# State space layer: softplus chain moved up by two to three turns; recurrent, distance and last layers' tiles turned by TensorE's transposing operation

## The chip, the cores and the metric

The kernel runs on one core of one Trainium2 chip. A core has five engines that run their own instruction streams: TensorE (PE in the profile, with its weight loads as PEld), VectorE (DVE), ScalarE (ACT), GpSimd (POOL) and SyncE (SP, which here only issues DMAs). SBUF is the working memory of 128 partitions, PSUM the memory that TensorE writes. The metric is the device time of one execution in microseconds (us).

## The reference

The model has four layers, each of which mixes tokens ("conv") and then works on each token ("ffn"), with a residual around both. The input x is 4 x 64 x 128 x 128 in float32; a row of 128 channels is a token. These are the parts that the change touches:

```python
# layers 0 and 2, ffn: a recurrence over all 8192 tokens of an image
Wx = einsum('bti,hi->bth', x, W)              # then batch norm over all tokens
yt = sigmoid(wx_t + yt @ V.T)                 # one step; scan over t
# layer 1, conv: distances between the rows of each image, from q = x - mean
score = -(q2[..., :, None] + k2[..., None, :] - 2.0 * einsum('bdnl,bdml->bdnm', q, k))
# layer 2, conv: a selective state space model, 128 channels x 16 states
dt = softplus(einsum('blr,dr->bld', dt, dt_proj_w) + dt_proj_b)
h = exp(dt_t * A) * h + (dt_t * x_t) * B_t    # one step; scan over all positions
y = einsum('bds,bs->bd', h, C_t)
# layer 3: pooled tokens for a graph (conv); a router over 64 experts (ffn)
logits = einsum('bsd,ed->bse', x, gate_w) + gate_b
```

Every one of these parts normalises the tokens first (mean and variance over the 128 channels), and the sums over channels need the tile with channels on the partitions, which is why tiles are turned.

## The kernel before, in words

**Turning a tile.** A token tile has 128 tokens on the partitions and 128 channels beside each other. The kernel turns it by a matmul of the tile, as the stationary operand, with the identity `env.ident`: the result in PSUM is the transposed tile. In float32 such a matmul is two passes over the array, so each call leaves two matmuls and two weight loads in the trace. Elsewhere the kernel already calls `transpose`, which leaves one of each (L541 and L623 of layer 0's mixer, L3405 and others of layer 3).

**Recurrent layers (0 and 2), `rnn_ffn`, L1157.** First the input pass, `rnn_inputs` (L1051): 16 blocks of 16 tiles. A block is loaded by SP, DVE takes the statistics, ACT, POOL and DVE scale the tiles, PE turns four tiles into one PSUM tile `pt` (`turn`, L1120) and multiplies four tiles with themselves into `gram` (`square`, L1126), and ACT copies `pt` to `xn`. Each buffer has two copies (`DEEP = 2`), so the load of a block waits until the last scaling of the block before last has read its buffer. Then the recurrence: the 8192 tokens of an image are cut into 128 chunks of 64 steps that run side by side, after 16 steps that warm the state up. A step computes z = xn[t] wt + state vt (L1233 and L1235, 512 columns each), ACT takes the sigmoid (L1239), and `give` (L1257) turns the four tiles of the state before (L1260), which DVE adds to the residual (L1261). On PE `give(t - 1)` stands between the matmuls of step t and those of step t + 1.

**The planner.** `rnn_inputs`, `l1_distances`, `l3_nodes` and the token pass of `l3_layer` write no order themselves: `Plan.step` (L66) is told an engine, a duration, what a step reads and writes and which buffers it takes, and `Plan.emit` (L94) lists the steps. For each engine it takes the first listed step that can start when the engine is free, by the durations it was told; the order that comes out is then fixed for PE, ACT, DVE and POOL. A changed duration can so change the order.

**Distances, `l1_distances`, L1700.** 16 blocks of 16 tiles: statistics, scaling, `turn` (L1790), copy to `xT` (L1797), then products of each turned tile with itself (L1806) on top of a diagonal (L1803), and the sum on DVE (L1813).

**State space layer, `l2_conv`, L2270.** 64 chunks of 512 positions x 2 images. The order is written out by hand in turns: turn t holds the scan of one pair of states (`one_state`, L2768 on DVE and the product gs, L2773 on POOL); a chunk has 32 turns. In a turn come first `decay` (da on ACT, for the scan three turns later), `spread` (bs on PE, every second turn), `fetch` (two cc DMAs on SP, every fourth turn), `inputs` (bs x dx on DVE, for the next turn), then the scan and gs; then the steps that `at(turn, ...)` has put on this turn; last, every second turn, `summed` (py on PE), for gs of five and six turns before. The steps of chunk n's projection are put on the 32 turns before the chunk is scanned, t0 = 32 (n - 1). The softplus chain is among them: `steps` (PE, L2589) and `parts` (ACT, L2593 and L2594) at t0 + 15 and 16, then

- `exp` (ACT, L2597), `one_more` (two on ACT, L2601 and L2602, which write w and less), `log` (ACT, L2605, in place on w),
- `lost` (POOL, L2608: e - less), `add_lost` (POOL, L2611: up + e), `size` (POOL, L2620: dt = w + up), `scaled` (POOL, L2623: dx = dt x xs),
- `twice(b, "dt")` and `twice(b, "dx")` (L2617): four DMAs on SP each, which lay the first (b = 0) or second image's half out for the scan. The first `inputs` of the chunk, on turn t0 + 31, needs dx of b = 0.

PE, ACT, DVE and POOL keep the order as written; the order of SP's DMAs is not written out. Other steps on the same turns: the previous chunk's `layer1` (PE, t0 + 18 and 21) and `hidden` (ACT, L2675, t0 + 19 and 22), `gelu` (ACT, t0 + 24).

**Last layer, `l3_layer`, L3109.** 16 blocks in the token pass: PE mixes four rows (L3170), DVE adds them to the loaded block (L3175) and takes statistics, POOL stores the block, the tiles are scaled into `xq` (L3189 and L3191), turned (`turn`, L3198), copied (L3204), multiplied with the gate (L3210) and written as logits by ACT (L3220). `l3_nodes` (L2880) turns one pooled tile for each of its 16 blocks (L2919).

Of the kernel before, what the change touches and what calls it, by code (L numbers as in the profile page):

```python
# [23 lines left out]
B, H, W, C = 4, 64, 128, 128  # L24
# [1026 lines left out]
def rnn_inputs(env, x, xn, gram):  # L1051


    nc, tc = env.nc, env.tc
    V, S, T, G = nc.vector, nc.scalar, nc.tensor, nc.gpsimd
    NB, DEEP = 16, 2
    with tc.tile_pool(name="rs", bufs=DEEP) as sb, tc.tile_pool(name="rp", bufs=3, space=PSUM) as psum:
        deep = ["xt", "st", "mv", "rs", "nb", "d", "t", "xl"]
        plan = Plan(dict(pt=3, **{n: DEEP for n in deep}), " ".join(deep))
        step = plan.step  # L1060

        def block(b, l0):
            v = {}
            plan.block()

            def load():
                v["xt"] = sb.tile([P, NB, C], F32, name="xt")
                nc.sync.dma_start(v["xt"], x[b, :, l0 : l0 + NB, :])

            def stats(j):  # L1070
                def f():
                    if j == 0:
                        v["st"] = sb.tile([P, NB, 2, 3], F32, name="st")
                    for q in range(j, j + 4):
                        V.bn_stats(v["st"][:, q].rearrange("p s k -> p (s k)"), v["xt"][:, q, :])
                return f

            def merge():
                d, v["mv"] = sb.tile([P, NB], F32, name="d"), sb.tile([P, NB, 2], F32, name="mv")
                mean, sq, mv = v["st"][:, :, :, 1], v["st"][:, :, :, 2], v["mv"]  # L1080
                V.tensor_sub(d, mean[:, :, 0], mean[:, :, 1])
                V.tensor_add(mv[:, :, 0], mean[:, :, 0], mean[:, :, 1])
                V.tensor_add(mv[:, :, 1], sq[:, :, 0], sq[:, :, 1])
                V.scalar_tensor_tensor(d, d, 0.25 * C, d, ALU.mult, ALU.mult)
                V.tensor_add(mv[:, :, 1], mv[:, :, 1], d)
                V.tensor_scalar(mv[:, :, 1], mv[:, :, 1], 1.0 / C, env.eps5, ALU.mult, ALU.add)

            def guess():
                v["rs"] = sb.tile([P, NB], F32, name="rs")
                S.activation(v["rs"], v["mv"][:, :, 1], AF.Ln)  # L1090
                S.activation(v["rs"], v["rs"], AF.Exp, scale=-0.5)
                if b == 0 and l0 == 0:
                    S.preload_act_table_set("natural_log_exp_and_others")

            def refine():
                r, t = v["rs"], sb.tile([P, NB], F32, name="t")
                V.tensor_mul(t, v["mv"][:, :, 1], r)
                V.scalar_tensor_tensor(t, t, -0.5, r, ALU.mult, ALU.mult)
                V.scalar_tensor_tensor(r, t, 1.5, r, ALU.add, ALU.mult)
                v["nb"] = sb.tile([P, NB], F32, name="nb")  # L1100
                V.scalar_tensor_tensor(v["nb"], v["mv"][:, :, 0], -0.5, r, ALU.mult, ALU.mult)

            def scale(eng, *js):
                def f():
                    if "xl" not in v:
                        v["xl"] = sb.tile([P, NB, C + 1], F32, name="xl")
                        G.memset(v["xl"][:, :, C : C + 1], 1.0)
                    for j in js:
                        r, n = v["rs"][:, j : j + 1], v["nb"][:, j : j + 1]
                        if eng is S:  # L1110
                            S.activation(v["xl"][:, j, 0:C], v["xt"][:, j, :], AF.Identity, bias=n, scale=r)
                        else:
                            eng.tensor_scalar(v["xl"][:, j, 0:C], v["xt"][:, j, :], r, n, ALU.mult, ALU.add)
                return f

            def turn(j0, w):
                def f():
                    w["pt"] = psum.tile([P, 4, P], F32, name="pt")
                    for j in range(4):
                        T.matmul(w["pt"][:, j, :], v["xl"][:, j0 + j, 0:C], env.ident, start=True, stop=True)  # L1120
                return f

            def square(j0):
                def f():
                    for j in range(j0, j0 + 4):
                        T.matmul(gram, v["xl"][:, j, 0:C], v["xl"][:, j, :], start=False, stop=False)  # L1126
                return f

            step("sp", 0.1, "", "xt", load, new="xt", late=4.0)
            for j in range(0, NB, 4):  # L1130
                step("dve", 1.15, "xt", "st", stats(j), new="st" if j == 0 else "")
            step("dve", 1.2, "st", "mv d", merge, new="mv d")
            step("act", 0.5, "mv", "rs", guess, new="rs")
            step("dve", 0.8, "mv rs", "rs nb t", refine, new="nb t")
            for j0 in range(0, NB, 4):
                w = {}
                if j0 % 8 == 0:
                    step(
                        "dve", 0.7, "xt rs nb" + " xl" * (j0 > 0), "xl" * (j0 == 0) + " xv%d" % j0, scale(V, j0, j0 + 4),
                        new="xl" if j0 == 0 else "",  # L1140
                    )
                step("pool", 0.5, "xt rs nb xl", "xp%d" % j0, scale(G, j0 + 3))
                step("act", 1.0, "xt rs nb xl", "xm%d" % j0, scale(S, j0 + 1, j0 + 2))
                ready = "xl xv%d xp%d xm%d" % (j0 - j0 % 8, j0, j0)
                step("pe", 1.0, ready, "pt", turn(j0, w), new="pt")
                step("pe", 1.05, ready, "", square(j0))
                step("act", 0.6, "pt", "", lambda j0=j0, w=w: S.copy(xn[:, l0 + j0 : l0 + j0 + 4, b, :], w["pt"]))

# [8 lines left out]
def rnn_ffn(env, x, out, w, vt, gamma, beta):  # L1157
# [4 lines left out]
    with tc.tile_pool(name="rc", bufs=1) as cp:  # L1162
# [63 lines left out]
        with tc.tile_pool(name="rw", bufs=4) as sb, tc.tile_pool(name="rx", bufs=4) as xp, tc.tile_pool(  # L1226
# [26 lines left out]
            def recurrence():  # L1253

                xt, state = None, start

                def give(t, done):  # L1257
                    pt = tp.tile([P, B, C], F32, name="pt")
                    for b in range(B):
                        nc.tensor.matmul(pt[:, b, :], done[:, b, :], env.ident, start=True, stop=True)  # L1260
                    nc.vector.tensor_add(xt[:, :, t % NO, :], xt[:, :, t % NO, :], pt)  # L1261
                    if t % NO == NO - 1:
                        for b in range(B):
                            nc.gpsimd.dma_start(ov[b, :, t + 1 - NO : t + 1, :], xt[:, b])

                for t in range(L):
                    new = last if t == L - 1 else sb.tile([P, B, NCH], F32, name="state")
                    sigmoid(new, cell(t, state))
                    if t > 0:
                        give(t - 1, state)  # L1270
                    if t % NO == 0:
                        xt = xp.tile([P, B, NO, C], F32, name="xo")
                        for b in range(B):
                            nc.sync.dma_start(xt[:, b], xv[b, :, t : t + NO, :])
                    state = new
                give(L - 1, last)
# [423 lines left out]
def l1_distances(env, x, dscr, keys):  # L1700
# [6 lines left out]
    with tc.tile_pool(name="dc", bufs=1) as cp, tc.tile_pool(name="ds", bufs=DEEP) as sb, tc.tile_pool(  # L1707
# [9 lines left out]
        def block(i):  # L1717
# [68 lines left out]
            def turn(j0, w):  # L1786
                def f():
                    w["pt"] = psum.tile([P, 4, P], F32, name="pt")
                    for j in range(4):
                        T.matmul(w["pt"][:, j, :], v["xl"][:, j0 + j, :], env.ident, start=True, stop=True)  # L1790
                return f

            def keep(j0, w):
# [476 lines left out]
def l2_conv(env, x, out, prm):  # L2270
# [14 lines left out]
    with ExitStack() as ctx:  # L2285
# [99 lines left out]
        def at(turn, *steps):  # L2385
            turns.setdefault(turn, []).extend(steps)
# [125 lines left out]
        def project(n, t0):  # L2512
# [124 lines left out]
            at(t0 + 13, lambda: part(N))  # L2637
            at(t0 + 15, steps)
            at(t0 + 16, parts)
            at(t0 + 17, exp)  # L2640
            at(t0 + 18, one_more)
            at(t0 + 19, lost)
            at(t0 + 20, log, load_res)
            at(t0 + 21, add_lost)
            at(t0 + 23, size, lambda: twice(0, "dt"))
            at(t0 + 26, scaled, lambda: twice(0, "dx"))
            at(t0 + 33, lambda: twice(1, "dt"))
            at(t0 + 34, lambda: twice(1, "dx"))

# [230 lines left out]
def l3_nodes(env, x, xl, poolT):  # L2880
# [4 lines left out]
    with tc.tile_pool(name="ns", bufs=DEEP) as sb, tc.tile_pool(name="np", bufs=2, space=PSUM) as psum:  # L2885
# [4 lines left out]
        def block(g, w0):  # L2890
# [25 lines left out]

            def turn():
                v["pt"] = psum.tile([P, P], F32, name="pt")
                T.matmul(v["pt"], v["p"], env.ident, start=True, stop=True)  # L2919

            def keep():
                S.activation(poolT[:, w0 // NB, g * P : g * P + P], v["pt"], AF.Identity, scale=1.0 / 16)
# [186 lines left out]
def l3_layer(env, x, out, cv, ff):  # L3109
# [7 lines left out]
    with ExitStack() as ctx:  # L3117
# [36 lines left out]
        with tc.tile_pool(name="go", bufs=DEEP) as sb, tc.tile_pool(name="gp", bufs=2, space=PSUM) as psum:  # L3154
# [4 lines left out]
            def block(g, w0):  # L3159
# [34 lines left out]
                def turn(w):  # L3194
                    def f():
                        w["pt"] = psum.tile([P, 4, P], F32, name="pt")
                        for j in range(4):
                            T.matmul(w["pt"][:, j, :], w["xq"][:, j, :], env.ident, start=True, stop=True)  # L3198
                    return f

                def keep(w):
# [33 lines left out]
                for j in range(0, NB, 4):  # L3235
# [1 line left out]
                    step("dve", 0.4, "xt y%d rs nb" % j, "xq xv", scale(V, w, j, 0), new="xq")  # L3237
                    step("pool", 1.0, "xt y%d rs nb xq" % j, "xp", scale(G, w, j, 1, 2))
                    step("act", 0.5, "xt y%d rs nb xq" % j, "xm", scale(S, w, j, 3))
                    step("pe", 1.2, "xq xv xp xm", "pt", turn(w), new="pt")  # L3240
                    step("act", 0.6, "pt", "xT", keep(w), new="xT")
                    step("pe", 1.0, "xT", "pl", gate(w), new="pl")
                    step("act", 1.0, "pl", lgn, logits(j, w), new=lgn if w0 + j == 0 else "")
# [268 lines left out]
```

## Time and profile before

| | us |
|---|---|
| three runs | 11602.66, 11594.26, 11613.55; median 11602.66 |
| the profiled execution | 11600.68 |
| its span, first to last instruction | 11598.8 |

Busy time over the span: DVE 9891.4 us (85%), ACT 7224.5 (62%), PE 6752.8 (58%), POOL 5633.8 (49%). Stages, in us from the span's start: input pass and recurrence of layer 0 about 1370 to 1720, distances 1727 to 1958, state space layer 6430 to 10550, input pass and recurrence of layer 2 about 10555 to 10905, last layer's token pass 11167 to 11460.

How to read it: a row of a timeline gives start, length, engine, line, operation, the tiles written and read, shapes and how many were merged into the row; in brackets stands how long the engine had been idle and what it waited for. Matmuls are pipelined and their ends are modelled, so how fast PE works is read from starts, not from busy time. "SPq" is SP issuing a DMA; the landing is seen in who waits for it. PEclk is the share of TensorE's clock that was granted.

### The profile page before, as it was taken

The numbers are of one execution on the slowest core, as the hardware profiler recorded it, in microseconds if no ns is written. First come the engines' busy times: TensorE is split into PE (matmuls) and PEld (weight loads), VectorE is DVE, ScalarE is ACT, GpSimd is POOL, SyncE is SP. The second block draws the span as 40 slices with busy tenths as digits, with TensorE's granted clock in tenths as the row PEclk, the third lists the DMA queues.
The fourth block names the chain that finished last, engine by engine and source line by source line (L and its number), as shares of the span: only waits on it lengthen the run. The fifth ranks groups of instructions, "written<-read, shape, count | busy, mean of one in ns | idle before, by whom it ended". The sixth has DMA issues, their size and how long they took to land. (4 is left out here: it accounts for less than half of the span.)

```text
span 11598.8 us, 117532 instructions
## 1 busy us (share of the span) xinstructions
PE 6752.8 (58%) x34862; PEld 4019.9 (35%) x34862; DVE 9891.4 (85%) x16377; ACT 7224.5 (62%) x9683; POOL 5633.8 (49%) x4762
## 2 busy tenths in 40 slices
PE   7877696000000000008999688888888888888675
PEld 5665564000000000007888233333333333335343
DVE  7567637999999999998998599999999999996444
ACT  4244434888886777743333587787788778775332
POOL 1000016999990000002332488888888888883322
PEclk8877798555555555559999788888888888888887
DMA  5312245111111111111111344444444444443444
GB/s 194 99 40 48 70 148 142 56 57 58 57 65 47 55 55 55 51 48 52 46 47 34 80 111 115 117 110 120 113 113 118 110 116 120 110 113 102 171 140 151
DMA packets 794209, 1059.52 MB, mean 91 GB/s; under 512 B 243564, under 2 KB 460878, under 8 KB 779982
## 3 DMA queue, kind: packets, MB, share of 16 engines
q1 hardware_dynamic: 749630, 925.61, 27.8%
q0 software_dynamic: 34368, 124.14, 3.2%
q8 instruction: 280, 4.59, 0.2%
q14 instruction: 379, 3.10, 0.1%
q10 hardware_dynamic: 9552, 2.08, 0.1%
HBM read 682.39 MB, written 251.71 MB: 81 GB/s over the span
## 5 line engine op out<-in xcount | busy, mean ns | idle before, releaser
L2773 POOL TENSOR_TENSOR gs<-hist,cc 128x512 f32<-128x512 f32 x2048 | 2586.7, 1272 | 659.9 <-DVE hist L2768 494.7
L2768 DVE TENSOR_TENSOR_SCAN hist<-da,state,bs 128x512 f32<-128x512 f32 x1984 | 2517.5, 1269 | 0.0
L1693 PE MATMUL pm<-ident,m 128*1 128x128 f32 x1 | 0.4, 372 | 3191.3 <-DMA pk<-spare 3191.3
L2729 ACT ACTIVATE da<-dt,am 128x512 f32<-128x512 f32 x2048 | 1420.6, 719 | 377.0 <-DVE hist L2768 320.9
L2760 DVE TENSOR_TENSOR bs<-dx,bs 128x512 f32<-128x512 f32 x2048 | 1380.8, 674 | 159.8 <-DMA dx<-dx 150.3
L1501 POOL TENSOR_TENSOR diff<-key 128x2048 f32<-128x2048 f32 (+11 forms) x364 | 1384.1, 3854 | 86.1 <-DVE key L1506 74.4
L2784 PE MATMUL py<-gs,both 128*64 128x512 f32 x4096 | 1253.1, 693 | 0.0
L1693 PEld LDWEIGHTS pm<-ident,m 128*1 128x1 f32 x1 | 0.1, 79 | 3191.4 <-issue 3191.4
L1523 ACT COPY keep<-rank 128x1536 int16<-128x1536 int16 (+11 forms) x364 | 612.8, 1686 | 437.5 <-DVE rank L1525 388.6
L1919 POOL IOTA row<- 72x1 int32 x1 | 0.1, 135 | 1769.8 <-ACTq L1868 1769.8
L1499 ACT COPY low<-key 128x2048 f32<-128x2048 f32 (+11 forms) x364 | 627.7, 1725 | 284.0 <-DVE key L1506 275.8
L1524 DVE COPY_PREDICATED rank<-back,rank 128x1536 int16<-128x1536 uint8 (+11 forms) x364 | 781.3, 2146 | 16.7 <-ACT keep L1523 16.7
L1525 DVE COPY_PREDICATED rank<-back,keep 128x1536 int16<-128x1536 uint8 (+11 forms) x364 | 777.8, 2137 | 12.5
L1506 DVE TENSOR_TENSOR key<-low,key 128x2048 f32<-128x2048 f32 (+11 forms) x364 | 744.4, 2045 | 12.4
L1505 DVE TENSOR_TENSOR key<-low,key 128x2048 f32<-128x2048 f32 (+11 forms) x364 | 749.0, 2058 | 6.3 <-DMA key<-dist 3.9
L2739 PE MATMUL bs<-bt,pick 96*128 96x512 bf16 x1024 | 435.1, 425 | 497.7 <-DVE hist L2768 492.3
L1502 ACT ACTIVATE turned<-diff 128x2048 int8<-128x2048 f32 (+11 forms) x364 | 600.4, 1699 | 36.6 <-DMA key<-dist 26.8
L1514 ACT ACTIVATE back<-turned 128x3072 uint8<-128x3072 int8 (+12 forms) x182 | 582.2, 3199 | 0.0
L2218 PE MATMUL pe<-ew,xg 128*128 128x128 f32 x4096 | 506.3, 277 | 0.0
L2218 PEld LDWEIGHTS pe<-ew,xg 128*128 128x128 f32 x4096 | 490.2, 194 | 4.0
L2784 PEld LDWEIGHTS py<-gs,both 128*64 128x64 f32 x4096 | 218.6, 146 | 693.7 <-issue 258.8
L2739 PEld LDWEIGHTS <-pick 96*128 96x128 bf16 x1024 | 98.9, 97 | 970.7 <-issue 970.7
(840 smaller groups left out, 17726.8 us busy)
## 6 DMA issues: line engine op xcount, KB each, us to landing
cc<-cd SPq DMA_DIRECT2D x1024, 256.0 KB
xt<-state SPq DMA_DIRECT2D x64, 1024.0 KB
dt<-dt SPq DMA_DIRECT2D x512, 128.0 KB
dx<-dx SPq DMA_DIRECT2D x512, 128.0 KB
xo<-state SPq DMA_DIRECT2D x128, 256.0 KB
state<-xo POOLq DMA_DIRECT2D x128, 256.0 KB, 2.8
xl<-in_L_ffn_weight SPq DMA_DIRECT2D x32, 1024.0 KB
tk<-in_x SPq DMA_DIRECT2D x32, 512.0 KB
```

Source lines behind the costliest of these rows:

```text
L1499: nc.scalar.copy(c, l)
L1501: nc.gpsimd.tensor_sub(d, lo[part], hi[part])
L1505: nc.vector.tensor_tensor(lo[part], c, hi[part], ALU.min)
L1506: nc.vector.tensor_tensor(hi[part], c, hi[part], ALU.max)
L1524: nc.vector.copy_predicated(l, t, h)
L1525: nc.vector.copy_predicated(h, t, kv)
L2218: T.matmul(w["pe"][:, j, :], w["xg"][:, q, j, :], ew[:, q, :], start=False, stop=(j == 3 and q == E - 1))
L2729: nc.scalar.activation(da, x_["dt%d" % b][:, s % 2, :], AF.Exp, scale=am[:, s : s + 1])
L2760: nc.vector.tensor_mul(live["db", t], x_["dx%d" % b][:, s % 2, :], live["bs", t - s % 2])
L2768: nc.vector.tensor_tensor_scan(h, live.pop(("da", t)), live.pop(("db", t)), 0.0 if first else state[b][:, s : s + 1], ALU.mult, ALU.add,)
L2773: nc.gpsimd.tensor_tensor(gs, h, live.pop(("cc", t)), ALU.mult)
L2784: nc.tensor.matmul(x_["py%d" % b][h * H : h * H + H], both, live.pop(("gs", t - 1 + h)), start=False, stop=(s == S - 1),)
```

## The change

Five turning matmuls become `transpose` calls with the same operands. In two places the planner is told a shorter duration for them: 0.55 for 1.0 in `rnn_inputs`, 0.7 for 1.2 in the last layer's token pass; in the distances and for the pooled tiles the told durations stay. In the state space layer seven compute steps of the softplus chain and the first image's copies move to earlier turns: `one_more` from 18 to 17, `lost` from 19 to 18, `log` from 20 to 18, `add_lost` from 21 to 20, `size` and the copies of dt from 23 to 21, `scaled` and the copies of dx from 26 to 23. `load_res` stays on turn 20, and the second image's copies on 33 and 34.

```diff
@@ rnn_inputs
-                        T.matmul(w["pt"][:, j, :], v["xl"][:, j0 + j, 0:C], env.ident, start=True, stop=True)
+                        T.transpose(w["pt"][:, j, :], v["xl"][:, j0 + j, 0:C], env.ident)
...
-                step("pe", 1.0, ready, "pt", turn(j0, w), new="pt")
+                step("pe", 0.55, ready, "pt", turn(j0, w), new="pt")
@@ rnn_ffn, give
-                        nc.tensor.matmul(pt[:, b, :], done[:, b, :], env.ident, start=True, stop=True)
+                        nc.tensor.transpose(pt[:, b, :], done[:, b, :], env.ident)
@@ l1_distances
-                        T.matmul(w["pt"][:, j, :], v["xl"][:, j0 + j, :], env.ident, start=True, stop=True)
+                        T.transpose(w["pt"][:, j, :], v["xl"][:, j0 + j, :], env.ident)
@@ l2_conv, project
             at(t0 + 16, parts)
-            at(t0 + 17, exp)
-            at(t0 + 18, one_more)
-            at(t0 + 19, lost)
-            at(t0 + 20, log, load_res)
-            at(t0 + 21, add_lost)
-            at(t0 + 23, size, lambda: twice(0, "dt"))
-            at(t0 + 26, scaled, lambda: twice(0, "dx"))
+            at(t0 + 17, exp, one_more)
+            at(t0 + 18, log, lost)
+            at(t0 + 20, load_res, add_lost)
+            at(t0 + 21, size, lambda: twice(0, "dt"))
+            at(t0 + 23, scaled, lambda: twice(0, "dx"))
@@ l3_nodes
-                T.matmul(v["pt"], v["p"], env.ident, start=True, stop=True)
+                T.transpose(v["pt"], v["p"], env.ident)
@@ l3_layer
-                            T.matmul(w["pt"][:, j, :], w["xq"][:, j, :], env.ident, start=True, stop=True)
+                            T.transpose(w["pt"][:, j, :], w["xq"][:, j, :], env.ident)
...
-                    step("pe", 1.2, "xq xv xp xm", "pt", turn(w), new="pt")
+                    step("pe", 0.7, "xq xv xp xm", "pt", turn(w), new="pt")
```

## The prediction

> **What bounds the kernel now.** I read the stage view first (busy time, TensorE clock and DMA share of stretches), because each part of the change lives in a stage with a limit of its own. The rows are the recurrent layer's input pass, its recurrence, the distances, the state space layer and the last layer's token pass; the columns are PE, PEld, DVE, ACT and POOL busy time with instruction counts, clock, DMA share, GB/s.
>
> ```profile
> 1370.00:1511.00 141.00, 120.87 (x1022) 118.32 (x1023) 94.14 (x482) 93.25 (x227) 30.34 (x80) 0.92 0.34 120
> 1554.00:1720.00 166.00, 164.53 (x762) 104.57 (x760) 45.23 (x67) 43.28 (x63) 32.56 (x61) 1.00 0.49 171
> 1727.00:1958.00 231.00, 179.16 (x1152) 140.16 (x1152) 173.95 (x579) 96.84 (x228) 117.81 (x145) 0.93 0.60 160
> 6430.00:10550.00 4120.00, 3457.98 (x13447) 1429.71 (x13448) 3903.41 (x4788) 3210.12 (x4705) 3352.23 (x3200) 0.86 0.43 112
> 11167.00:11460.00 293.00, 206.79 (x786) 119.79 (x786) 177.37 (x581) 139.60 (x296) 81.20 (x154) 0.85 0.42 153
> ```
>
> PE alone is full in the recurrence (164.5 of 166 us), DVE alone in the state space layer (3903 of 4120). In the other three nothing is full, so they turn on loops between engines. The recurrence and the input pass come twice in the kernel.
>
> Next I asked what DVE waits for in the state space layer (total us, times, longest):
>
> ```profile
> DVE bs L2760 <- DMA dx<-dx: 150.3, 55, 46.4
> DVE bs L2760 <- PE bs L2739: 9.2, 15, 1.8
> ```
>
> One wait stands out: 46.4 us once, at the start, and 103.9 us over 54 later chunks, 1.9 us each. The timeline of one chunk shows where it comes from (start, length, engine, line, operation, wait):
>
> ```profile
> 7998.99 1.28 POOL L2773 TENSOR_TENSOR gs<-hist,cc 128x512 f32<-128x512 f32 x1 [0.49 <-PE pa L2670]
> ...
> 8002.13 2.36 POOL L2608 TENSOR_TENSOR e<-e,less 128x1024 f32<-128x1024 f32 x1
> 8006.91 2.35 POOL L2611 TENSOR_TENSOR up<-up,e 128x1024 f32<-128x1024 f32 x1
> 8011.81 2.36 POOL L2620 TENSOR_TENSOR dt<-w,up 128x1024 f32<-128x1024 f32 x1
> 8014.14 3.72 POOL L2773 TENSOR_TENSOR gs<-hist,cc 128x512 f32<-128x512 f32 x3
> 8017.83 2.35 POOL L2623 TENSOR_TENSOR dx<-dt,xs 128x1024 f32<-128x1024 f32 x1
> 8020.21 2.39 SPq L2617 DMA_DIRECT2D dx<-dx  x4
> 8023.20 0.69 DVE L2760 TENSOR_TENSOR bs<-dx,bs 128x512 f32<-128x512 f32 x1 [2.21 <-DMA dx<-dx]
> ```
>
> POOL ends dx at 8020.18, its copies land 3.02 us later, and DVE has idled since 8020.99.
>
> Last, one step of the recurrence, and a group that already uses the transposing operation:
>
> ```profile
> 1603.34 1.02 PE L1235 MATMUL z<-state,vt_sb 128*128 128x512 f32 x2
> 1604.20 1.05 PE L1260 MATMUL pt<-ident,state 128*128 128x128 f32 x8
> 1604.40 0.69 ACT L1239 ACTIVATE state<-z,bias 128x512 f32<-128x512 f32 x1 [1.92 <-PE z L1235]
> 1605.09 1.02 PE L1233 MATMUL z<-xn,wt 128*128 128x512 f32 x2
> ```
>
> ```profile
> 475.96 0.60 PE L623 MATMUL p<-ident,om 128*49 128x128 f32 x4
> ```
>
> Four turning matmuls are eight passes, 0.89 us (1604.20 to 1605.09), 0.111 each. Four transposing operations are four passes; with 0.272 us for one (the least duration at L623), (0.60 - 0.272) / 3 = 0.109 us from one to the next. So a turned tile costs half.
>
> **The change part by part.** All sums go against the profiled execution: span 11598.8, time 11600.7, which is 2 us under the median shown.
>
> *Recurrence (twice).* A step lasts 2.61 us (1603.34 to 1605.95, the next z<-state). It loses four passes: 4 x 0.111 = 0.445, leaving 2.165. The cover is the sigmoid: it ends at 1605.09 and its reader starts at 1605.95, 0.86 us of slack, of which 0.41 remain. The same loop without turning, in the warm-up steps, runs at 1.90 us (1536.52, 1538.42, 1540.32), below 2.165; so PE stays the limit. DVE's addition (0.69 us) and the loads and stores (DMA share 0.49, going to 0.59) fit. Gain 64 x 0.445 x 2 layers = 57 us. Bounds: the only four 128-column transposes in a row, of a strided source at L3405, take 0.75 us, so (0.75 - 0.284) / 3 = 0.155 each and a gain of 35; 0.109 gives 58. I take 57, since L1260 reads whole rows.
>
> The Trainium skill ("TensorE: Matmul & The Clock Gate", Terms) calls the transposing mode four times faster for FP32. By that a tile would cost 0.222 / 4 = 0.055 us and the two recurrences would gain 85. The row at 475.96 shows a factor of two.
>
> *State space layer.* Nothing is added; instructions change places. On ACT, L2601 and L2602 now follow L2597 without the da between, and L2605 comes two turns earlier, ahead of the four L2675. The three start 0.94 and 1.07 apart from 7996.83, so "less" ends at 8000.0. On POOL the first step now stands behind gs of turn 18 (ends 8000.27), so it starts there and doesn't wait. From it to dx there stood, in issue spacing, the steps 2.32 + 2.31 + 2.33, seven gs at 1.23 and a state copy of 0.14: 15.7 us. Now five gs and two copies stand between: 6.96 + 6.11 + 0.28 = 13.35. So dx starts at 8013.6 and ends at 8016.0, 4.2 us earlier; it lands at 8019.0, 2.0 before DVE is free. The 2.2 us wait goes.
>
> What each queue is moved past: SP issues the four dt copies (2.43 us) as POOL ends dt, now at 8011.0, and the cc fetch behind them waits for POOL's state copy at 8013.6 anyway, then dx at 8016.0: no collision. load_res keeps its turn. ACT's da for turn 21 now stands behind L2601 and L2602 and ends at 8000.6 against 7998.5; its scan starts at about 8002.9, so 2.3 us of lead remain, and the next two da lose one L2605 (1.06). The first L2675 group moves back by as much, and with it PE's second layer1, which waits for its bank; the bs behind that is asked for four turns later. POOL is up to 5.9 us behind DVE after dx where it was 4.7; PE waits for gs (5 turns of 1.77 later), so bs comes later. From a gs to the bs it can hold up lie eight turns, 14.2 us; gs, two py matmuls of 0.86 and bs need about 5, so POOL may lag 8 to 9 us before DVE feels it. Late next on DVE is nothing: scans follow at 1.77 us (8012.34, 8014.10, 8015.88). Gain 104 (the 103.9 us); the first 46.4 is a chain without scans between and stays. Bounds: 50, if half the wait returns by a late da or bs; 115, if the ACT wait for dt (48.7 us in 63) also counted.
>
> *Input pass (twice).* PE falls from 7.1 to 5.3 us per block of 7.5, but PE is not the loop: the load of a block is issued when the last scaling by ACT frees its buffer (ACT 1431.28 + 0.88, SP 1432.22), DVE waits for it (0.64), and so on over two blocks, 15.04 us. The planned duration 0.55 for 1.0 changes the written order: the planner's turn now ends before ACT's second scaling does, so ACT's first copy precedes the third scaling and the second the fourth. One more copy stands ahead of the last scaling, 0.46 us (1438.34 to 1438.80) per loop, 8 loops, 2 layers: +7.4. The tail of 16 tiles saves 1.8 each: -3.6. I take +4; bounds -10 (a third of the 33 us that ACT's copies wait for PE) and +10.
>
> *Distances.* The order stays. DVE waits 10.6 us for the products and 35.7 for loads. I take -4 (tail 1.8, 2 of the waits); bounds -14 and +10 (five more clock windows of 3.4 us at half speed).
>
> *Last layer.* SP's load waits for ACT's scaling, which stands behind copies that wait for PE; each block loses 0.445 us there, some 11 blocks: -5. Bounds -30 (half of the 53.7 us that DVE waits for loads) and +10 (the new order puts one 0.58 us copy ahead in 16 blocks). The 16 pooled tiles lie beside DMA: 0.
>
> Sum: -57 - 104 + 4 - 4 - 5 = -166; 11600.7 - 166 = 11435.
>
> **The rivals.**
> *Half the wait returns* in the state space layer (dx late by SP's order, or da late in turns 21 to 23): 11600.7 - 166 + 52 = 11487. For it: the margins are 2.0 and 2.3 us. Against: every step's cover has a row.
> *The turned tiles cost as before* (the transposing form of a whole tile gives nothing): 11435 + 57 = 11492. Against it: one pass per call at L623 and L541.
> *POOL's lag stops DVE* (slower): the four long steps now fall within 16 us on POOL, gs slips, PE's py waits, the bs behind it comes late. It decides once DVE waits over 162 / 63 = 2.6 us per chunk, which needs POOL's lag beyond some 11 us at turn 24; at 4 us per chunk the time is 11435 + 252 = 11687. For it: PE already waits 234.6 us for gs. Against: the lag I work out is 5.9.
> *The clock falls* where transposes replace matmuls, if they count for nothing: the passes then take twice as long, PE becomes the limit, and a block needs 10.7 us for 7.5 in the input passes (3.2 x 15 x 2 = 96), 17.5 for 13 in the distances (4.5 x 15 = 68), 17.2 for 15 in the last layer (2.2 x 16 = 35); 11435 + 199 = 11634. Against it: from 324.4 to 327.8 us, 16 of 20 matmuls are transposes of L623, and the granted clock is 1.00 there and through 331.2. In the recurrence matmuls alone fill 1.72 of 2.165 us.
> By the Trainium skill (the same page, Part 4: PE-mode transpose) transposing doesn't count as PE-busy and full clock does not engage; the clock at 324.4 speaks against that.
>
> **How the numbers follow.** Chances: the forecast 0.76, half the wait 0.10, tiles as before 0.03, POOL's lag 0.06, the clock 0.03, nothing measurable 0.02. The forecast's own range is 11385 to 11475 (its bounds: all gains at their best give -215). Taking in the two cases near 11490 makes 11385 to 11500, with over 8 in 10. Faster 0.89, within 0.2% (23 us, what a measurement here can tell) 0.02, slower 0.09.
>
> **What would show it.** Right: recurrence steps of 2.16 us with four passes at L1260; no row of DVE waiting for dx but the first; first scans of successive chunks 58.3 us apart, where they are 60.8 now in three chunks of four. Wrong: DVE waiting for bs from PE or scans waiting for da; steps of 2.6; a clock under 0.9 in the input pass.

## The result and the profile after

| | before | after |
|---|---|---|
| median, us | 11601.4 (11594.26 to 11613.55) | 11411.9 (11396.1 to 11417.72) |
| profiled execution, us | 11600.68 | 11396.1 |
| its span, us | 11598.8 | 11394.3 |

The ratio is 0.9833, 95% interval 0.9816 to 0.985: 190 us faster between the medians, where 166 were forecast. The time 11411.9 lies 23 us under the forecast 11435 and inside the forecast's own range of 11385 to 11475.

The stage view of the changed kernel (stretch in us, its length, then PE, PEld, DVE, ACT, POOL busy with instruction counts, granted clock, DMA share, GB/s); the stretches are the input pass and the recurrence of layer 0, the distances, the state space layer, and the last layer's token pass:

```profile
1367.50:1511.50 144.00, 98.24 (x764) 93.17 (x765) 94.08 (x480) 93.99 (x226) 31.49 (x80) 0.86 0.33 118
1554.00:1692.00 138.00, 136.40 (x508) 72.31 (x506) 44.87 (x66) 43.77 (x64) 32.28 (x61) 1.00 0.58 206
1699.50:1928.00 228.50, 164.11 (x896) 118.93 (x896) 174.00 (x579) 95.36 (x228) 118.47 (x145) 0.87 0.60 161
6402.00:10430.00 4028.00, 3450.62 (x13452) 1427.75 (x13452) 3910.02 (x4794) 3206.46 (x4706) 3351.12 (x3200) 0.87 0.45 114
11014.00:11258.00 244.00, 168.68 (x531) 80.44 (x530) 173.23 (x581) 141.32 (x296) 83.03 (x154) 0.87 0.51 184
```

The limits are where they were: PE is full in the recurrence (136.4 of 138), DVE in the state space layer (3910 of 4028), nothing elsewhere. Two lengths stand out: the recurrence's stretch is 28 us shorter, and the token pass takes 244 us where it took 293.

One step of the recurrence in the changed kernel (start, length, engine, line, operation):

```profile
1599.90 1.02 PE L1235 MATMUL z<-state,vt_sb 128*128 128x512 f32 x2
...
1600.76 0.60 PE L1260 MATMUL pt<-ident,state 128*128 128x128 f32 x4
...
1602.06 1.02 PE L1235 MATMUL z<-state,vt_sb 128*128 128x512 f32 x2
```

Four passes instead of eight, and 2.16 us from one step to the next (1599.90 to 1602.06), where it was 2.61.

What DVE waits for in the state space layer now (us in total, times, longest):

```profile
DVE bs L2758 <- DMA dx<-dx: 46.7, 3, 45.4
DVE res L2693 <- PE pn L2686: 25.4, 16, 14.5
...
DVE bs L2758 <- PE bs L2737: 5.9, 11, 1.6
```

The wait for dx is there once, at the start (45.4), and 1.3 us besides; before it was 46.4 and 103.9.

From the first and last instruction of each stage in the two profiled executions:

| part | forecast | measured |
|---|---|---|
| recurrence, two layers | -57 | -28.4 and -28.3 |
| state space layer | -104 | -95.5 (4125.3 to 4029.8) |
| input pass, two layers | +4 | +3.4 and -0.5 |
| distances | -4 | -2.1 |
| last layer | -5 | -51.8 (422.5 to 370.7) |
| pooled tiles | 0 | -1.2 |

In these two executions the change is 204 us, where it is 190 between the medians. Four terms came out about as worked out (recurrence, input pass, distances, pooled tiles). The last layer gained ten times its term, and the state space layer lost something the working did not contain.

### The profile page after: what moved, and what is told of

The parts are those of the page before. It is cut to its first block, busy times and chain, and to the rows that moved or that the text cites. A ratio compares the mean times of both kernels' runs of the same rounds, so it can differ in the third digit from the quotient of the medians.

```text
span 11394.3 us, 114467 instructions
## 1 busy us (share of the span) xinstructions
PE 6576.2 (58%) x33310; PEld 3832.9 (34%) x33310; DVE 9893.7 (87%) x16377; ACT 7223.3 (63%) x9683; POOL 5638.0 (49%) x4762
## 5 line engine op out<-in xcount | busy, mean ns | idle before, releaser
L2758 DVE TENSOR_TENSOR bs<-dx,bs 128x512 f32<-128x512 f32 x2048 | 1382.0, 675 | 53.2 <-DMA dx<-dx 46.7
```

What stands on the lines that cost most here:

```text
L2758: nc.vector.tensor_mul(live["db", t], x_["dx%d" % b][:, s % 2, :], live["bs", t - s % 2])
```

## The experiments

The theory for the state space layer and the recurrence is that of the prediction. For the last layer there are two: A, the shorter told duration changes the written order of the token pass and the order makes the gain; B, the faster turning makes it.

### The softplus chain alone

```diff
 (the kernel before, with these turns only)
-            at(t0 + 23, size, lambda: twice(0, "dt"))
-            at(t0 + 26, scaled, lambda: twice(0, "dx"))
+            at(t0 + 21, size, lambda: twice(0, "dt"))
+            at(t0 + 23, scaled, lambda: twice(0, "dx"))
...
```

> The kernel before with the moved softplus chain alone. If the chain alone makes the whole change of the state space layer (its stretch went from 4125.3 to 4029.8 us in the two profiles shown), this kernel is 95 us faster, ratio 0.992, and the layer's stretch is 4030 us. If the other edits help the layer from outside (its first wait, the clock), it gains less than 80 us. If the prediction's 104 us were lost to a wait for the moved steps, DVE waits for bs or da in this trace; if they were lost in the statistics chunks (every fourth), those chunks are 70.0 us apart and the others 58.5.

Measured: 11494.16 us, ratio 0.9904 (0.9889 to 0.992). From the layer's first scan to its last it took 3908.2 us, for 4006.4 before and 3911.7 in the changed kernel: the chain alone makes the change of this layer, 98 us. The time fell by 114; of the rest, 11 us lie in the first stage, which the edit does not touch. First scans of successive chunks are 58.5 us apart (60.8 before; 58.3 were forecast), but in every fourth chunk, which takes the statistics of the next group, it is 69.9 (68.5 before; all medians). Over the layer, the 48 other chunks gave 111 us, and the 15 statistics chunks cost 13, 0.9 us each on the mean. In the changed kernel it is 109 and 14.

Where the 0.9 us go is seen on POOL and DVE in the same 8 us of the changed kernel, first POOL and then DVE:

```profile
8069.57 2.51 POOL L2771 TENSOR_TENSOR gs<-hist,cc 128x512 f32<-128x512 f32 x2
8072.02 0.19 POOL L2773 COPY state<-hist 128x4 f32<-128x4 f32 x1
8072.17 2.35 POOL L2623 TENSOR_TENSOR dx<-dt,xs 128x1024 f32<-128x1024 f32 x1
8074.48 2.48 POOL L2771 TENSOR_TENSOR gs<-hist,cc 128x512 f32<-128x512 f32 x2
```

```profile
8070.89 1.23 DVE L2414 TENSOR_TENSOR d<-st 128x16 f32<-128x16 f32 x1
8072.04 0.21 DVE L2415 TENSOR_TENSOR mv<-st 128x16 f32<-128x16 f32 x1
8072.17 2.39 DVE L2416 TENSOR_TENSOR v<-st 128x16 f32<-128x16 f32 x1
8074.49 1.28 DVE L2417 SCALAR_TENSOR_TENSOR d<-d 128x16 f32<-128x16 f32 x1
8075.81 1.19 DVE L2418 TENSOR_TENSOR v<-v,d 128x16 f32<-128x16 f32 x1
8077.03 0.23 DVE L2419 TENSOR_SCALAR v<-v,eps 128x16 f32<-128x16 f32 x1
```

DVE's operations on 16 numbers per partition last as long as the POOL operation beside them: L2416 begins with dx at 8072.17 and ends at 8074.56, dx at 8074.52. Over the layer, 71 of these operations begin while POOL is idle and take 0.18 us on the mean; 89 begin while a POOL operation runs and take 1.18; the long ones end within 0.03 us (median) of a start or end of a POOL operation. Meanwhile bs (L2758), which reads one operand from PSUM, keeps its 0.675 us. The six merging operations take 5.64 us from first start to last end in the changed kernel (4.12 before), since POOL's backlog now covers their turn; the four refining ones take 1.67 (2.63 before), since it no longer covers theirs: together 0.6 us more. DVE's wait for the residual (L2693 <- PE) grew from 21.3 to 25.4 us over the whole layer, in waits of some 0.3 us in 12 of the statistics chunks, 0.3 per chunk. These two are the 0.9 us.

By the Trainium skill ("SBUF — State Buffer", Who interferes with whom), a VectorE instruction with two SBUF inputs and a GpSimd instruction that reads SBUF exclude each other for a whole instruction, and one with at most one SBUF input, outside VectorE's two-port modes, goes free. The trace agrees, with 1.18 against 0.18 us. It is a rule that spoke against this change, and the prediction did not weigh it.

### The recurrence alone

```diff
-                        nc.tensor.matmul(pt[:, b, :], done[:, b, :], env.ident, start=True, stop=True)
+                        nc.tensor.transpose(pt[:, b, :], done[:, b, :], env.ident)
```

> The kernel before with the transposing operation in the two recurrences alone. By the prediction's working: 57 us faster, 28.5 us for each recurrence, steps of 2.165 us, ratio 0.995. By the rule of a fourth of the price for float32: 85 us, steps of 1.94. If a step is held by ACT's sigmoid or DVE's addition once PE is shorter, it stays above 2.3 us and the gain is under 40 us.

Measured: 11547.81 us, ratio 0.9952 (0.9937 to 0.9967), so 60 us; the stages are 28.3 and 29.6 us shorter. Steps, in this kernel's trace:

```profile
1605.43 1.02 PE L1235 MATMUL z<-state,vt_sb 128*128 128x512 f32 x2
1606.29 0.60 PE L1260 MATMUL pt<-ident,state 128*128 128x128 f32 x4
1607.59 1.02 PE L1235 MATMUL z<-state,vt_sb 128*128 128x512 f32 x2
```

2.16 us. The factor of two holds and PE stays the limit; the factor of four is refuted for these tiles.

### The last layer: order alone, operation alone

```diff
 (order alone)
-                    step("pe", 1.2, "xq xv xp xm", "pt", turn(w), new="pt")
+                    step("pe", 0.7, "xq xv xp xm", "pt", turn(w), new="pt")
 (operation alone)
-                            T.matmul(w["pt"][:, j, :], w["xq"][:, j, :], env.ident, start=True, stop=True)
+                            T.transpose(w["pt"][:, j, :], w["xq"][:, j, :], env.ident)
```

> The kernel before with the last layer's told duration 0.7 for 1.2 alone: the tiles are still turned by matmul, only the written order of the token pass changes. Theory A (the order carries the gain: loads of tiles and ACT's scalings stand ahead of other work): the last layer's stretch falls by some 45 of the 52 us, ratio 0.996. Theory B (the shorter turning carries it): the stretch stays within 5 us, ratio 1.000. Theory C (both are needed): under 15 us here and under 15 us with the transposing operation alone, and 52 us only together.

> The kernel before with the transposing operation in the last layer's token pass alone, told duration 1.2 kept: the order on every engine is that of the kernel before. Theory A (order): the last layer's stretch falls by 5 us or less, as the prediction had it. Theory B (speed of the turning): it falls by some 45 us, ratio 0.996. Theory C (both are needed): under 15 us.

Measured: the order alone gives 11566.45 us, ratio 0.9965 (0.9951 to 0.9978), and the last layer's stage is 38 us shorter. The operation alone gives 11603.48, ratio 0.9996 (0.9987 to 1.0005), and the stage is 8 us shorter. A holds: the order carries three quarters of the gain, with tiles turned as slowly as ever.

How it does so is a matter of buffers. A block of 16 tiles sits in one of three buffers from its load until its last scaling, and the load of the third next block waits for that scaling. In the kernel before, around the load of block 7, which takes the buffer of block 4 (SP's issue of a weight load, POOL's store of block 6, POOL's scalings, SP's load of the tile, DVE's first addition of the loaded block):

```profile
11245.37 0.38 SPq L3378 DMA_DIRECT2D xl<-in_L_ffn_weight  x1
...
11246.36 0.58 POOL L3179 DMA_DIRECT2D out<-xt  x1 [7.61 <-DVE xq L3191]
11246.98 2.63 POOL L3191 TENSOR_SCALAR xq<-xt,rs,nb 128x128 f32<-128x128 f32 x6
...
11247.88 0.32 SPq L3165 DMA_DIRECT2D xt<-state  x1
...
11257.26 1.28 DVE L3175 TENSOR_TENSOR xt<-xt,ps 128x512 f32<-128x512 f32 x2 [5.53 <-DMA xt<-state]
```

The last scaling of block 4 is the second in POOL's row of six. It ends at 11247.85 (ACT's last one at 11247.38), and the load follows at once. In the written order this scaling stands behind the store of block 6, and the store needs all four additions of block 6; DVE's own last scaling of block 4 stands behind the fourth of them (11245.38), too. So each load waits until the block loaded before it has been added to completely. The load lands 9.3 us later, and DVE idles 5.53 us for it. The same block with the order alone changed:

```profile
11246.38 0.32 SPq L3165 DMA_DIRECT2D xt<-state  x1
...
11248.17 0.58 POOL L3179 DMA_DIRECT2D out<-xt  x1 [1.56 <-PE pt L3198]
...
11251.43 0.69 DVE L3175 TENSOR_TENSOR xt<-xt,ps 128x512 f32<-128x512 f32 x1 [1.75 <-POOL xq L3191]
```

POOL's last scaling of block 4 now stands ahead of the store of block 6 and ended at 11240.62. DVE's stands behind the second addition of block 6, not the fourth. ACT's is the last, at 11246.31, and the load follows it. It lands 4.9 us after its issue, at 11251.31. DVE waits for it here as well: the row names POOL's scaling only because that ended last, at 11251.39. Over the first 13 blocks, the ones whose buffer a later load takes, POOL's scaling is the last in 11 before, and ACT's in 11 with the new order.

From load to last scaling, blocks 3 to 7 hold their buffers 37.0, 37.2, 42.1, 47.3 and 53.4 us before, and 32.7, 31.4, 32.7, 33.3 and 35.2 with the new order. A third of the last figures, 17.8 and 11.7, is about what separates two loads (11247.9 to 11266.0 is 18.1; 11246.4 to 11257.9 is 11.5). DVE's waits for the loads fall from 53.7 us in 13 to 37.9 in 8. With the operation as well, in the changed kernel, the blocks hold 29.8, 28.7, 29.7, 32.0 and 33.6.

Part of this may be the weight loads. SP issues one of 1 MB 2.5 us ahead of each tile load from block 7 on in the kernel before, and eight of these nine tiles are first used 8 to 10 us after their load, where those of blocks 3 to 6 took 5.7 to 7.1. With the new order six of the nine still have a weight load up to 3 us ahead, and five of these took 7.6 to 10.3 us; the three without took 4.7 to 5.1. Blocks 3 to 6 have no weight load ahead in either kernel and differ nevertheless (37 to 47 us against 31 to 33). From the load of block 3 to that of block 7 the new order saves 6 us (49.1 to 42.8), from there to the load of block 15 it saves 24 (149.7 to 125.4). How much of these 24 is due to the weight loads was not tried.

### The input passes: operation alone, order alone

```diff
 (operation alone)
-                        T.matmul(w["pt"][:, j, :], v["xl"][:, j0 + j, 0:C], env.ident, start=True, stop=True)
+                        T.transpose(w["pt"][:, j, :], v["xl"][:, j0 + j, 0:C], env.ident)
 (order alone)
-                step("pe", 1.0, ready, "pt", turn(j0, w), new="pt")
+                step("pe", 0.55, ready, "pt", turn(j0, w), new="pt")
```

> The kernel before with the transposing operation in the two input passes alone, told duration 1.0 kept, so that the written order is that of the kernel before. By the prediction's working only the tail of 16 tiles gains: 1.8 us for each pass, 3.6 in all, ratio 0.9997. If ACT's copies, which wait 33 us for PE in the kernel before, get their tiles sooner throughout, each pass falls by 5 us or more.

> The kernel before with the input passes' told duration 0.55 for 1.0 alone, tiles still turned by matmul. By the prediction's working one more copy of ACT stands ahead of the last scaling, 0.46 us in each of 8 loops, so each pass is 3.7 us longer, 7.4 in all, ratio 1.0006. If the order is harmless and something else lengthened the first pass in the changed kernel (141.2 to 144.6 us), both passes stay within 1 us.

Measured: the operation alone gives 11596.39 us, 0.9995 (0.9986 to 1.0005); from the first load to the last turned tile the passes take 137.6 and 133.0 us for 140.7 and 138.9. The order alone gives 11646.23, 1.004 (1.0025 to 1.0054); the passes take 164.2 and 162.1, 23 us more each. Blocks follow each other in 9.0 us, for 7.5. ACT's rows show why, first the kernel before and then the order alone:

```profile
1448.80 0.59 ACT L1147 COPY xn<-pt 128x512 f32<-128x512 f32 x1 [1.12 <-PE pt L1120]
1449.28 0.22 ACT L1090 ACTIVATE rs<-mv 128x16 f32<-128x16 f32 x1
1449.53 0.22 ACT L1091 ACTIVATE rs<-rs 128x16 f32<-128x16 f32 x1
1450.58 0.58 ACT L1147 COPY xn<-pt 128x512 f32<-128x512 f32 x1 [0.84 <-PE pt L1120]
1451.07 2.42 ACT L1111 ACTIVATE xl<-xt,nb,rs 128x128 f32<-128x128 f32 x6
```

```profile
1454.88 0.58 ACT L1147 COPY xn<-pt 128x512 f32<-128x512 f32 x1 [1.20 <-PE pt L1120]
1455.36 0.22 ACT L1090 ACTIVATE rs<-mv 128x16 f32<-128x16 f32 x1
1455.61 0.22 ACT L1091 ACTIVATE rs<-rs 128x16 f32<-128x16 f32 x1
1456.77 1.65 ACT L1111 ACTIVATE xl<-xt,nb,rs 128x128 f32<-128x128 f32 x4 [0.94 <-DVE nb L1101]
```

Before, the root of the next block (L1090) stands ahead of the last copy, and by the time that copy is done DVE has refined the root: the scalings start without a wait. In the new order the root stands behind the last copy. So the loop runs through everything: last copy, root, DVE's refining (ACT waits 0.94), scaling, four turns on PE, last copy. With turns of 0.89 us it costs 1.5 us per block, 47 us in the two passes. With turns of half that the same order costs much less: the changed kernel's passes (144.1 and 138.2) are 12 us longer than with the operation alone, and 6 us longer than in the best kernel below, which has the fast turning without the new order (140.8 and 135.1). So the two edits act on each other. For the order, 7.4 us were worked out, near its cost with the fast turning, and 40 short of it with the slow one; for the turning 3.6 were worked out, where it gives 9 by itself and 44 once the order is in place.

### The margin of dx

```diff
 (the changed kernel)
-            at(t0 + 23, scaled, lambda: twice(0, "dx"))
+            at(t0 + 25, scaled, lambda: twice(0, "dx"))
```

> The changed kernel with dx and its copies two turns later, on 25 for 23. The prediction put the landing of dx 2.0 us before DVE is free. Two turns are two gs on POOL, 2 x 1.23 = 2.46 us, so 0.5 us of the wait should be back in each chunk without statistics (47): DVE waits for dx 20 to 30 us more and the layer is 20 to 30 us longer, ratio against the kernel before 0.985 to 0.986. If the margin is larger than worked out, nothing returns (0.983); if POOL's backlog moves with the step and dx lands 3.5 us later or more, 1.5 us return in each chunk, 70 us.

Measured: 11449.06 us, ratio 0.9872 (0.9856 to 0.9889), 37 us slower than the changed kernel. The wait is back:

```profile
DVE bs L2758 <- DMA dx<-dx: 78.7, 50, 45.2
```

78.7 us in 50, for 46.7 in 3: 32 us, 0.7 in each of 47 more chunks. The spacing goes from 58.5 to 59.6, and the layer is 48 us longer from first scan to last (3959.9 for 3911.7), where 20 to 30 were expected: DVE also waits 7 us more for bs from PE (12.9 for 5.9) and 6 more for the residual (31.0 for 25.4). The margin of the changed kernel is 2.46 - 0.7 = 1.8 us if dx slides by two gs; 2.0 had been worked out. Its own trace agrees: DVE first uses dx 4.8 us after POOL has ended it, and the copies take 3.0 us to land.

### Statistics moved ahead of POOL's long steps

```diff
 (the changed kernel; first edit)
-                at(t0 + 9 + j, lambda j=j: stats(j))
-            at(t0 + 25, merge)
-            at(t0 + 26, root)
+                at(t0 + 9 + j // 2, lambda j=j: stats(j))
+            at(t0 + 17, merge)
+            at(t0 + 18, root)
```

> The changed kernel with the statistics of the next group read two per turn (turns 9 to 16 for 9 to 24), and DVE's six small merging operations on turn 17 for 25 and ACT's root on 18 for 26. Theory: these operations of 128x16 are slow (6.29 us for six in the changed kernel) because they fall where POOL works off its four long steps; on turn 17 no long step runs, they take 2.5 us or less, and 16 groups gain 3.8 us or more each: 60 us, the statistics chunks 66 us apart for 70.0, ratio against the kernel before 0.978. Rival: they are slow wherever POOL runs anything, or DVE then waits at the next place: gain under 15 us, ratio 0.982 to 0.983.

Measured: 11392.44 us, ratio 0.9819 (0.9803 to 0.9835): 20 us under the changed kernel, not 60, and 11 us from the first scan to the last (3900.4 for 3911.7), so the rival's bound of 15 us holds. Merging fell from 5.64 to 1.89 us per group (means over the 16 groups, from first start to last end; the 6.29 of the expectation is a typical group), as the theory had it, but refining, left on turn 29, grew from 1.67 to 4.78:

```profile
L2430 DVE TENSOR_TENSOR t<-t,v 128x16 f32<-128x16 f32 x16 | 36.8, 2301 | 0.6
L2429 DVE SCALAR_TENSOR_TENSOR t<-rs 128x16 f32<-128x16 f32 x16 | 30.2, 1889 | 0.5 <-ACT rs L2424 0.5
```

(Columns: busy time in all, mean ns of one, idle before it.) Two operations that take 0.15 and 0.175 us in the changed kernel take 1.9 and 2.3 here. DVE comes to them sooner, and POOL has not worked off its backlog yet: the delay had not gone but moved to the next operations of the kind.

```diff
 (both outside POOL's backlog; and the input passes' told duration back at 1.0)
-            at(t0 + 4, start)
-                at(t0 + 9 + j, lambda j=j: stats(j))
-            at(t0 + 25, merge)
-            at(t0 + 26, root)
-            at(t0 + 29, refine)
+            at(t0, start)
+                at(t0 + 5 + j // 2, lambda j=j: stats(j))
+            at(t0 + 13, merge)
+            at(t0 + 14, root)
+            at(t0 + 17, refine)
...
-                step("pe", 0.55, ready, "pt", turn(j0, w), new="pt")
+                step("pe", 1.0, ready, "pt", turn(j0, w), new="pt")
```

> The changed kernel with two edits: the whole of the statistics ahead of POOL's long steps (load on turn 0 for 4, statistics two per turn on 5 to 12 for 9 to 24, DVE's merging on 13 for 25, ACT's root on 14 for 26, DVE's refining on 17 for 29), and the input passes' told duration back at 1.0. Theory: small DVE operations are slow only where POOL runs without a pause, from its first long step (turn 18) until its backlog is gone; merging alone moved out of it fell from 6.29 to 2.05 us for each group, but refining, still inside, grew from 1.66 to 4.67. With both outside, the two take 3.2 us or less for 7.95, so 16 groups gain 76 us or more in the state space layer; the input passes gain 3 to 7 us each. Together some 85 us, ratio against the kernel before 0.976. Rival: the stretching only moves on to other DVE operations, which are then slower: gain under 30 us in the layer.

Measured: 11367.69 us, ratio 0.9785 (0.9769 to 0.9802) against the kernel before, the best of all, where 0.976 was expected. It is 44 us under the changed kernel by the medians and 56 by the two ratios, since the kernel before took 11617.92 us in this comparison, 16 more than in that of the result; 85 were expected. From the first scan to the last it is 3874.9 for 3911.7, 37 us; the statistics chunks are 67.0 apart for 70.0. The input passes take 140.8 and 135.1 us for 144.1 and 138.2. Two things kept the rest:

```profile
DVE st L2408 <- DMA xt<-state: 26.9, 16, 7.5
...
L2417 DVE SCALAR_TENSOR_TENSOR d<-d 128x16 f32<-128x16 f32 x16 | 18.9, 1184 | 0.0
L2431 DVE SCALAR_TENSOR_TENSOR rs<-t,rs 128x16 f32<-128x16 f32 x16 | 16.2, 1011 | 0.6
L2419 DVE TENSOR_SCALAR v<-v,eps 128x16 f32<-128x16 f32 x16 | 14.5, 907 | 0.6
```

The statistics come so early that DVE waits for their load in each group (20 us more in all). And merging takes 2.61, refining 1.67: L2417 and L2431 still meet a gs in 15 of 16 groups, and L2419 a POOL operation of the normalising step (L2498, 1.09 us). The theory was too narrow: these short POOL operations hold them up as well, by the rest of their length, and the long steps and the backlog only make a meeting likelier and longer.

### Two more edits on top

```diff
 (the kernel of the last experiment; l1_blocks)
-                        T.matmul(w["pt"][:, j, :], v["xl"][:, j0 + j, :], env.ident, start=True, stop=True)
+                        T.transpose(w["pt"][:, j, :], v["xl"][:, j0 + j, :], env.ident)
 (l3_layer)
-                    step("pe", 0.7, "xq xv xp xm", "pt", turn(w), new="pt")
+                    step("pe", 0.45, "xq xv xp xm", "pt", turn(w), new="pt")
```

> The kernel of e10_stats_first with two more edits: the turned tiles of the first attention blocks (the stage with 2048 turning passes) by the transposing operation, its told duration 1.0 kept; and the last layer's told duration 0.45 for 0.7. In the first, PE is busy 1062 of 1240 us and loses 1024 passes of 0.111 us, 114 us; DVE is busy 1096, so at most some 75 us can come out, and if PE waits less for DVE's work it already waits for, 20 to 40 are likelier; 0 if the loop there is DVE's. In the second: if the order that the shorter told duration writes is what shortens the time that a tile's buffer is held, a still shorter one may shorten the token pass further, by up to 15 us, or lengthen it; if only the true length of the turning matters, it stays within 3 us.

Measured: 11397.07 us, ratio 0.9812 (0.9795 to 0.9828): 29 us slower than without these edits. The attention blocks take 1137.0 us for 1125.1 from their first turned tile to their last, though PE has fewer passes to do; ACT's waits for the turned tiles fall from 147.0 to 107.5 us against the changed kernel, but a wait of PE for DVE's tile g (L2158) comes up (39.4), and ACT's waits for DVE's e grow from 98.7 to 120.7. What closes that loop was not followed further, and why it grew by 12 us stays open. The last layer, its graph part included, is 16 us longer than with 0.7 (448.7 for 432.7). The kernel of the last experiment has the changed kernel's order in this stage and took 7 us more there (432.7 for 425.6), so some 7 of the 16 may be spread between executions. A told duration closer to the measured one (0.44 us for the four turns) did not write a better order.

## Why the prediction was right, and where not

**Recurrence** (57): right in every step. Four passes instead of eight, 2.16 us per step for 2.165, 56.7 us; alone, 58 by its stages.

**State space layer** (104): the mechanism was right. POOL's lag after dx, counted from a gs behind DVE's scan, is 6.0 us at turn 24 for 5.9; the leads of da in turns 21 to 23 are 2.0 to 2.8 for 2.3; the 103.9 us of waits are 1.3. The step that failed is "Late next on DVE is nothing". It looked at scans only, in a chunk without statistics. In every fourth chunk DVE's merging operations on turn 25 stand beside the backlog, and these 15 chunks grew by 0.9 us on the mean, 14 us. The 48 others gave 109 us, 2.3 each, where the wait alone had been 2.2, so that about 95 remained of 104.

**Input pass** (+4): the sum held (+2.9), but the working behind it was incomplete, and that its errors cancel is luck. One more copy does stand ahead of the last scaling. The same order also puts the root behind the last copy, which the working did not see, and with that the cost of the order depends on the turning: 47 us with the old one, 6 to 12 with the new one, for 7.4. The turning gives 9 by itself, for 3.6.

**Distances** (-4): -2.1, inside its bounds. No experiment took it by itself.

**Last layer** (-5): the failed term, sized at a tenth, and beyond its bound of -30. Its first sentence was about right in size: each block loses 0.445 us of turning where the load waits, 5 us; the operation alone gives 8. It took ACT's scaling for the one that the load waits for; POOL's ends up to 0.5 us after it in most blocks. But the changed order was priced only as a possible loss ("puts one 0.58 us copy ahead"), by one block's row, without following how long a block then holds its buffer. The last scaling that frees a buffer came out from behind the store and the fourth addition of a later block, and that order was worth 38 us. The two alone make 46 of the 52 us; the rest is within what the stage varies by between executions (7 us).

**The range.** The parts' gains at their best add up to 227 us (58, 115, 10, 14 and 30), not to the 215 from which the range's lower end was taken.

**The rivals.** Half the wait's return and POOL's lag stopping the scans did not come: DVE's waits for bs from PE are 5.9 us, for 9.2. The clock did fall. The prediction named a clock under 0.9 in the input pass as a sign of being wrong, and it is 0.86 in the pass of layer 0, where it was 0.92; in the distances it is 0.87, for 0.93. What the rival made of it did not follow: most blocks of the pass come 7.3 to 7.5 us apart, not 10.7, with a fourth fewer matmuls on PE. With the operation alone the clock of that pass is 0.88, with the order alone 0.92, so the fall comes with the operation. But PE is also less busy with it (98.2 of 144 us, for 120.9 of 141), and which of the two lowers the clock stays open. In the recurrence it is 1.00, and transposes fill a fifth of PE's time there (0.445 of 2.16 us). By the Trainium skill ("TensorE: Matmul & The Clock Gate", Part 4: PE-mode transpose) transposes do not count as busy and do not bring the full clock. In the recurrence the other passes alone could hold it, and no run here had transposes alone, so the runs do not settle it.

## What to carry over

A duration told to a planner is an edit of the whole written order, and must be priced by itself: over the loop through the buffers (how long a block holds one), and by what moves behind the last copy, not by one row. Here the same kind of edit was worth -38 us in one stage and +47 in two others, while halving the true cost of the turning gave 8 and 9 by itself. Two edits of one loop must be priced together as well: with the faster turning the 47 were 6 to 12. When a chain is moved earlier on one engine, ask which small operations of another engine now fall beside its backlog, above all in the chunks that are not like the one that was looked at.

## What was not expected of the hardware

A DVE operation with both inputs in SBUF waits until the POOL operation beside it ends, and the trace shows this as length and not as idle time: 0.18 us when it begins beside an idle POOL, 1.18 on the mean beside a busy one. It can wait for several in a row: the longest, L2415 at 7580.12 in the changed kernel, took 4.92 us and ended with the second gs after dx. L2419, whose second operand is one number per partition, is held up in the same way (0.95 us beside L2498, for 0.23). The waits view has no row for it. It is found by comparing the mean duration of one shape in two places: 0.175 us for L2430 in the changed kernel and 2.301 with merging moved away.
